# Graph attention layers 2 and 3: four heads projected ahead, the other pairs of heads projected inside the attention, and the order of its runs

## The chip, the cores and the metric

The kernel runs on one core of a Trainium2 chip. The metric is the device time in microseconds of one execution. The times shown are the median of three executions, and the profile is one further execution, recorded instruction by instruction. The engines of the core are TensorE (PE, matmuls and transposes, writing to PSUM), VectorE (DVE), ScalarE (ACT), GpSimd (POOL) and SyncE (SP, which only issues transfers). They run beside one another and wait for each other through semaphores; each takes its own instructions in order. Transfers are issued from the queues of SP, ACT and POOL.

## What is computed

Four graph layers over the same 2708 nodes with 512 features, each added to its input and layer-normalised. Layers 2 and 3 are graph attention (GAT) layers with eight heads of 64 features, and they are what the change touches:

```python
def _L2_gnn_ref(h, adj, W, a):                       # heads of layer 2; those of layer 3 are alike
    Wh = jnp.einsum('ni,hio->hno', h, W)             # [8 heads, 2708, 64]
    f1 = jnp.einsum('hno,ho->hn', Wh, a[:, :64])
    f2 = jnp.einsum('hno,ho->hn', Wh, a[:, 64:])
    e = jax.nn.leaky_relu(f1[:, :, None] + f2[:, None, :], 0.2)
    attention = jax.nn.softmax(jnp.where(adj[None] > 0, e, NEG_INF), axis=-1)
    h_prime = jnp.einsum('hnm,hmo->hno', attention, Wh)
    return jnp.transpose(h_prime, (1, 0, 2)).reshape(h.shape[0], 512)

x = _layernorm(x + layer2(x, adj))
# layer 3: elu(heads), then one attention with a single head of 512, elu, and an MLP 512 -> 1024 -> 512
x = _layernorm(x + layer3(x, adj))
```

All of it is float32. Layers 0 and 1 are aggregation layers without attention.

## The kernel before

The nodes are cut into 22 tiles of 128 rows (`NT`), the last with 20 rows. The program runs through stages: layers 0 and 1, then for each of layers 2 and 3 a projection (`project`) and the attention of its eight heads (`heads_attention`), then the projection, the attention and the MLP that end layer 3.

**The projection** (`project`, L588) goes tile by tile. It fetches 128 rows of x (`source`; for layer 3 that is `summed`, L950, which reads layer 2's heads from DRAM, scales them by the inverse divisors, adds the input, makes the layer norm and stores the result from POOL's queue, L961). PE turns them by four transposes (L131) and ACT copies the turned rows to SBUF (`xT`, L133; two buffers in the pool `ahead`). Then eight matmuls (L643), four slices of 128 features by two halves of the heads, accumulate into two PSUM tiles `pm` of 256 features and 8 more columns each: the halves' extra columns are the two attention scalars of each node. A float32 matmul is two instructions on PE, so a tile has 16 of them. From the scalars, DVE takes `dcol` and `b` (L648, L650), ACT makes the exponentials `ecol`, `ucol` (L664, L665) and `vcol` (L678), POOL makes `bcol` (L679), and PE turns `b` so that `v` can be stored as rows in DRAM (`keep_v`, L622 and L623). Two DVE instructions of 256 columns (L672) scale the features by `ecol` into `R2`, which stays in SBUF: [128 rows, 22 tiles, 512 features]. In the last six tiles, some of the first attention instructions are made ahead (`att.first`, L734: five in layer 2, four in layer 3).

**The attention** (`heads_attention`, L759) has eight runs. A run is a block of target nodes (11 tiles, 1408 columns, or the other 11, 1300 columns) by a pair of heads. The order before is block by block, and pair by pair within a block:

```python
runs = [(b, h0) for b in range(len(att.blocks)) for h0 in range(0, H, 2)]
```

At the start of a run SP loads `v` of each head, spread over the partitions (`v_bc`, L716, three buffers). The run has 22 steps, one for each tile j of neighbours. In a step DVE makes the masked weights e = max(v, u) * mask for each of the two heads (L722, five buffers, one instruction for each head, [128, 1408] or [128, 1300]); ACT makes from e the part above the leak's bend (`c`, L749, eleven buffers); and PE adds R2's features times e into `po` (L916), three PSUM tiles of up to 512 columns with the two heads on the two halves of the array's columns: 12 instructions a step. After every fourth step PE adds up the divisors from `c` (L818). In the first run of each block, the same sums are made once for the mask alone (`products`, L801, at steps 12, 16 and 20 of the run before it, or of the run itself for block 0). What is left of a run is spread over the first steps of the next (`finish`, the dictionary `todo`): the last divisors, folding them (L790), dividing (L840 to L845), and in layer 2 turning the heads to rows (L851) and storing them to DRAM in `o_dram` (L861 and after).[...]

PE's order is written out by hand: each instruction that goes through `pe()` is put behind the one before. The order on the other engines follows from a scheduler with the program's order as its priority, and from the pools: a tile's buffer is free when its last reader has ended. `summed` for the first two tiles and `elu_turned` (L966, the source of the projection after layer 3) for the first three can start while the attention still runs, since block 0 is complete after the fourth run; `elu_turned` is called from the last run's steps 9, 13 and 17.

## Time and profile before

| | us |
|---|---|
| median of three executions | 2957.79 (2957.10 to 2959.47) |
| span of the profiled execution | 2955.5 |
| layer 2: projection | 868 to 958 |
| layer 2: attention of the heads | 958 to 1504 |
| layer 3: projection | 1504 to 1608 |
| layer 3: attention of the heads | 1608 to 2155 |
| layer 3: the rest | 2155 to 2955 |

The stages' ends are read from the first and last instructions of their lines. The windows of these stages give the busy time of each engine:

```profile
core 0 of [0], span 2955.5 us
core 0: us, PE busy (x) PEld busy (x) DVE busy (x) ACT busy (x) POOL busy (x), PEclk, DMA share, GB/s
868.00:958.00 90.00, 89.73 (x453) 74.56 (x453) 37.48 (x122) 27.24 (x107) 9.20 (x31) 1.00 0.29 85
958.00:1504.00 546.00, 533.58 (x3782) 222.84 (x3781) 535.88 (x414) 508.44 (x412) 3.67 (x3) 1.00 0.12 40
1504.00:1608.00 104.00, 99.33 (x494) 79.05 (x493) 75.06 (x235) 45.42 (x135) 31.98 (x66) 0.97 0.55 178
1608.00:2155.00 547.00, 529.24 (x3723) 221.36 (x3721) 536.45 (x415) 509.60 (x399) 6.06 (x10) 1.00 0.12 41
```

After the stretch and its length, each pair is the busy time of an engine and (x) its number of instructions; PEld is PE's loading of weights, which goes on beside the matmuls. PEclk is the granted clock, DMA share the mean busy share of the 16 DMA engines. Two warnings for reading it. Matmuls are pipelined and their ends are modelled, so a busy PE need not be a PE at its limit; the time from one start to the next tells more. And the two attentions take 1093 of 2955 us; their runs, from one copy of the run's result (ACT, L926) to the next, last 75.7, 68.5, 69.8 and 73.0 us for block 0 of layer 2 and 63.9 to 65.5 us for block 1, and nearly the same in layer 3.

### The profile page before, as it was taken

The page shows a single profiled execution, that of the slowest core. Times are in us where ns is not written, and L with a number is a line of the kernel's source. Part 1 is how long each engine was busy: PE and PEld are TensorE (multiplying, and loading weights), DVE is VectorE, ACT ScalarE, POOL GpSimd, SP SyncE. Part 2 cuts the span into 40 slices and gives each one's busy share as a digit, 9 for nine tenths or more (in the row PEclk, how much of TensorE's full clock was granted, in tenths as well). Part 3 has the DMA queues.
Part 4 walks back from the last instruction along what each step waited for, and adds up shares of the span by engine and source line. Part 5 has one row for each costly group of instructions (what it writes and reads, how often), then busy time and mean ns, then how long its engine had stood idle before and what let it go on. Part 6 is the DMA issues. An engine that isn't in the chain of part 4 may idle for free. (4 is left out here: it accounts for less than half of the span.)

```text
span 2955.5 us, 36461 instructions
## 1 busy us (share of the span) xinstructions
PE 2874.1 (97%) x14398; PEld 1606.6 (54%) x14398; DVE 1998.5 (68%) x2408; ACT 1515.0 (51%) x1759; POOL 207.4 (7%) x344
## 2 busy tenths in 40 slices
PE   8999999999999999999999999999999999999998
PEld 4557766458888343444466433444475555555555
DVE  5866637543334999999977999999953434444342
ACT  3646532113223999999965999999951000000001
POOL 1101101101110000000022000000000010000001
PEclk9999999999999999999999999999999999999999
DMA  4633426322222111111143111121161000000000
GB/s 128 130 87 72 107 79 185 118 65 86 83 72 82 35 40 39 38 45 44 35 138 134 40 40 39 41 65 37 33 157 61 4 25 15 25 15 16 15 20 22
DMA packets 121152, 185.59 MB, mean 63 GB/s; under 512 B 41741, under 2 KB 66562, under 8 KB 120972
## 3 DMA queue, kind: packets, MB, share of 16 engines
q1 hardware_dynamic: 91808, 121.57, 13.8%
q0 software_dynamic: 18160, 57.39, 6.8%
q10 hardware_dynamic: 11004, 4.22, 0.6%
q8 instruction: 115, 1.88, 0.3%
q14 instruction: 65, 0.53, 0.1%
HBM read 153.10 MB, written 44.65 MB: 67 GB/s over the span
## 5 line engine op out<-in xcount | busy, mean ns | idle before, releaser
L722 DVE SCALAR_TENSOR_TENSOR e<-v_bc,ucol,maskT 128x1408 f32<-128x1408 f32 (+3 forms) x804 | 1135.9, 1469 | 327.6 <-PE pn L1097 314.4
L749 ACT ACTIVATE c<-e,bcol 128x1300 fp8e4<-128x1300 f32 (+1 forms) x688 | 965.8, 1423 | 65.4 <-DVE e L722 21.8
L916 PE MATMUL po<-e,R 128*64 128x512 f32 (+2 forms) x4224 | 907.8, 549 | 30.2 <-DVE e L722 27.3
L916 PEld LDWEIGHTS po<-e,R 128*64 128x64 f32 x4224 | 343.0, 137 | 561.9 <-issue 387.2
L1097 PE MATMUL pn<-e,R 128*128 128x512 f32 (+1 forms) x1056 | 413.4, 542 | 0.0
L1097 PEld LDWEIGHTS pn<-e,R 128*128 128x128 f32 x1056 | 191.0, 190 | 199.3 <-issue 196.1
L1048 ACT ACTIVATE w<-pl,b 128x256 f32<-128x256 f32 (+1 forms) x88 | 41.0, 466 | 372.8 <-PE pl L1046 364.7
L478 PE MATMUL acc<-yH,kT 128*128 128x512 f32 x484 | 197.4, 408 | 4.6 <-ACT kT L351 4.6
L478 PE MATMUL acc<-yL,kT 128*128 128x512 f32 x484 | 189.2, 391 | 0.0
L529 PE MATMUL acc<-yH,mf 128*128 128x512 f32 x484 | 188.4, 389 | 0.0
L529 PE MATMUL acc<-yL,mf 128*128 128x512 f32 x484 | 188.3, 389 | 0.0
L643 PE MATMUL pm<-w,xT 128*128 128x264 f32 (+1 forms) x704 | 167.5, 391 | 2.4 <-POOL ln_rs L120 0.8
L244 PE MATMUL pm<-weight,xT 128*128 128x512 f32 (+1 forms) x344 | 158.3, 603 | 7.6 <-DVE u L334 6.8
L1046 PE MATMUL pl<-lin 128*128 128x256 f32 (+1 forms) x704 | 153.4, 371 | 3.7 <-DVE lin L945 3.7
L120 POOL TENSOR_TENSOR ln_rs<-ln_rs,half 128x1 f32<-128x1 f32 (+1 forms) x88 | 55.1, 627 | 1447.1 <-DVE ln_rs L119 1378.6
L1071 PE MATMUL pl<-lin,w 128*128 128x512 f32 x336 | 150.8, 593 | 0.0
L1046 PEld LDWEIGHTS pl<-lin 128*128 128x128 f32 x704 | 129.1, 190 | 34.5 <-issue 15.8
L526 ACT CAST mf<-maskT 128x1024 fp32r<-128x1024 fp8e4 (+1 forms) x66 | 64.5, 977 | 156.5 <-PE acc L529 152.9
L643 PEld LDWEIGHTS pm<-w,xT 128*128 128x128 f32 (+1 forms) x704 | 129.2, 189 | 27.7 <-ACT xT L133 3.0
L244 PE MATMUL pm<-w,xT 128*128 128x512 f32 x296 | 135.3, 600 | 6.0 <-DVE yL L230 3.1
L351 ACT ACTIVATE kT<-maskT 128x512 fp32r<-128x512 fp8e4 (+1 forms) x132 | 77.5, 593 | 118.1 <-PE acc L478 118.1
L818 PE MATMUL pd<-c,parts_c 128*12 128x384 fp8e4 (+2 forms) x2752 | 128.3, 307 | 0.0
(239 smaller groups left out, 2635.4 us busy)
## 6 DMA issues: line engine op xcount, KB each, us to landing
rows<-x_dram SPq DMA_DIRECT2D x63, 256.0 KB
v_bc<-v_dram SPq DMA_DIRECT2D x16, 704.0 KB
rows<-in_x_dram SPq DMA_DIRECT2D x42, 256.0 KB
x_dram<-u POOLq DMA_DIRECT2D x42, 256.0 KB, 2.4
v_bc<-v_dram SPq DMA_DIRECT2D x16, 650.0 KB
m<-in_adj_dram POOLq DMA_DIRECT2D x13, 677.0 KB, 6.9
r_dram<-u POOLq DMA_DIRECT2D x21, 256.0 KB, 2.3
rows<-r_dram SPq DMA_DIRECT2D x21, 256.0 KB
```

The source lines that it names most:

```text
L244: order(nc.tensor.matmul(pm[:n], xT[:, k, :n], w[:, k, :], start=(k == 0), stop=(k == KD - 1)))
L351: made = nc.scalar.activation(kT[:, :w], maskT[:, j, b[0] * P:b[0] * P + w], AF.Relu, scale=-1.0)
L478: nc.tensor.matmul(pa[t], kT[:, (t - b[0]) * P:(t - b[0] + 1) * P], y[:, j, :], start=(j == 0 and y is yH), stop=(j == NT - 1 and y is yL))
L529: nc.tensor.matmul(pa, mf[:, j - g0, :], y[:, j, :], start=(j == 0 and y is yH), stop=(j == NT - 1 and y is yL))
L643: nc.tensor.matmul(pm[a][:m, :D // 2 + heads], xT[:, k, :m], w[:, k, a, :D // 2 + heads], start=(k == 0), stop=(k == KD - 1))
L722: self.made = nc.vector.scalar_tensor_tensor(e[:, :w], v[:, :w], ucol[:, j, h:h + 1], maskT[:, j, c0:c0 + w], op0=OP.max, op1=OP.mult)
L749: nc.scalar.activation(c[:, :w], e[:, :w], AF.Sigmoid, bias=bcol[:, j, h:h + 1], scale=STEP, saturate=False)
L818: pe(nc.tensor.matmul(p[32 * g:32 * g + 12, :c1 - c0], parts_c[:, j, h, :], c[:, c0:c1], start=(i == 0 and h == hs[0]), stop=(i == NT - 1 ...
L916: pe(nc.tensor.matmul(po[i][HO * k:HO * k + HO, :c1 - c0], R2[:, j, h * HO:(h + 1) * HO], e[:, c0:c1], start=(i_ == 0), stop=(i_ == NT - 1)))
L1046: nc.tensor.matmul(pl[:, :w], self.lin1[:, k, f * P:(f + 1) * P], h[:, k, :w], start=(k == 0), stop=(k == KD - 1))
L1071: nc.tensor.matmul(pl[:n], gT[:, f, (t - t0) * P:(t - t0) * P + n], self.lin2[:, f, :], start=(f == 0), stop=(f == KF - 1))
L1097: nc.tensor.matmul(pn[k][:, :w], R2[:, j, k * P:(k + 1) * P], e[:, :w], start=(j == 0), stop=(j == NT - 1))
```

## The change

For layers 2 and 3:

- `project` makes the features of heads 0 to 3 alone, with all sixteen attention scalars: one PSUM tile of 272 columns, four matmuls a tile (8 instructions), one scaling into `R2`. Half of the weights are loaded.
- Each tile's turned rows `xT` are stored to a new DRAM tensor `xT_dram`, from POOL's queue.
- The attention's runs go pair by pair: both blocks of heads 0 and 1, then both of heads 2 and 3, and so on. The sums of the masks are made in the first run for block 0 and in the second for block 1.
- The features of heads 4 and 5 are made during runs 1 to 3 and those of heads 6 and 7 during runs 4 to 6 (`projected`), in eight, eight and six tiles. For each tile SP loads its turned rows into a buffer (`rows`, three of them), PE makes four matmuls of 128 columns (8 instructions) at one of the steps 1, 3, 5, 7, 12, 14, 16, 18, and a DVE instruction scales four tiles at once from PSUM (512 columns) at step 11 and at the first step of the next run. The weights of the pair are loaded from SP at the first of the three runs.
- `ps_t` has one buffer instead of two; its bank goes to the features' PSUM tile `ps_p`.
- `elu_turned` for the first three tiles is called at steps 14, 17 and 20 of layer 3's last run.

Block 0 is now complete after the seventh run. In the order of instructions that follows, DVE's work of `summed` for the first two tiles lies at the start of layer 3's projection, where before it lay within layer 2's attention.

```diff
@@ -89,6 +89,11 @@
 
     o_dram = dram.tile([N, D], F32, name="o_dram")
     oT_dram, rc_dram = [], []
+    xT_dram = dram.tile([2, NT, P, KD * P], F32, name="xT_dram")
+
+    def turned_rows(layer, t, n):
+        return xT_dram[layer, t].rearrange("p (k n) -> p k n", k=KD)[:, :, :n]
+
 
 
 
@@ -592,12 +597,20 @@
 
         w = weight_tile()
         hh = max(heads // 2, 1)
-        for k in range(KD):
-            for a in range(2):
-                src = (w_src[4 * a:4 * a + 4, k * P:(k + 1) * P, :].rearrange("h p o -> p h o") if heads > 1 else
-                       w_src[k * P:(k + 1) * P, a * D // 2:(a + 1) * D // 2].rearrange("p (h o) -> p h o", h=1))
-                nc.scalar.dma_start(w[:, k, a, :D // 2].rearrange("p (h o) -> p h o", h=hh), src)
-        nc.gpsimd.tensor_copy(w[:, :, :, D // 2:D // 2 + heads], wa[:, layer, :, :, :heads])
+        half_d = D // 2
+        if heads > 1:
+            w = w.rearrange("p k a c -> p (k a c)")[:, :KD * (half_d + 2 * H)].rearrange("p (k c) -> p k c", k=KD)
+            for k in range(KD):
+                nc.scalar.dma_start(w[:, k, :half_d].rearrange("p (h o) -> p h o", h=hh),
+                                    w_src[:hh, k * P:(k + 1) * P, :].rearrange("h p o -> p h o"))
+            nc.gpsimd.tensor_copy(w[:, :, half_d:].rearrange("p k (i h) -> p k i h", i=2), wa[:, layer])
+            pieces = [w]
+        else:
+            for k in range(KD):
+                for a in range(2):
+                    nc.scalar.dma_start(w[:, k, a, :half_d], w_src[k * P:(k + 1) * P, a * half_d:(a + 1) * half_d])
+            nc.gpsimd.tensor_copy(w[:, :, :, half_d:half_d + heads], wa[:, layer, :, :, :heads])
+            pieces = [w[:, :, a, :half_d + heads] for a in range(2)]
         with ExitStack() as ph:
             sm = ph.enter_context(tc.tile_pool(name=f"{name}_s", bufs=2))
             ps_tr = ph.enter_context(tc.tile_pool(name=f"{name}_ptr", bufs=2, space=PSUM))
@@ -629,7 +642,9 @@
                 xT = xTs(t)
                 if t + 1 < NT:
                     xTs(t + 1)
-                pm = [ps_mm.tile([P, D // 2 + H], F32, name=f"pm{a}") for a in range(2)]
+                pm = [ps_mm.tile([P, half_d + 2 * H], F32, name=f"pm{a}") for a in range(len(pieces))]
+                s_ = pm[0][:, half_d:half_d + heads]
+                d_ = pm[0][:, half_d + H:] if heads > 1 else pm[1][:, half_d:half_d + heads]
 
                 twice = heads > 1 and t == LAST
                 if twice:
@@ -639,33 +654,33 @@
                     nc.gpsimd.memset(R2[TWIN:2 * TWIN, LAST, :], 0.0)
                 m = TWIN + n if twice else n
                 for k in range(KD):
-                    for a in range(2):
-                        nc.tensor.matmul(pm[a][:m, :D // 2 + heads], xT[:, k, :m], w[:, k, a, :D // 2 + heads],
+                    for a, piece in enumerate(pieces):
+                        nc.tensor.matmul(pm[a][:m, :piece.shape[2]], xT[:, k, :m], piece[:, k, :],
                                          start=(k == 0), stop=(k == KD - 1))
+                if heads > 1:
+                    nc.gpsimd.dma_start(turned_rows(layer, t, m), xT[:, :, :m])
                 if t:
                     keep_v(t - 1)
                 d = dcol[:n, t, :heads]
-                nc.vector.tensor_copy(d, pm[1][:n, D // 2:D // 2 + heads])
+                nc.vector.tensor_copy(d, d_[:n])
                 b = bs[t] = sm.tile([P, H], F32, name="b")
-                nc.vector.tensor_scalar(b[:n, :heads], pm[0][:n, D // 2:D // 2 + heads], -RANGE, RANGE,
-                                        op0=OP.max, op1=OP.min)
+                nc.vector.tensor_scalar(b[:n, :heads], s_[:n], -RANGE, RANGE, op0=OP.max, op1=OP.min)
...
                 else:
                     nc.scalar.activation(ecol[:n, t, :heads], d, AF.Exp, scale=ALPHA)
                     nc.scalar.activation(ucol[:n, t, :heads], d, AF.Exp, scale=1.0 - ALPHA)
                 with tc.issue_after(scaled[t - 1].ins) if first and t else nullcontext():
                     made = first(t) if first else None
-                for a in range(0 if twice else 2):
+                for a in range(0 if twice else len(pieces)):
...
@@ -756,7 +771,7 @@
         oT_dram.append(dram.tile([D, (z - a) * P], F32, name=f"oT_dram{i}"))
         rc_dram.append(dram.tile([H, 12 * P], F32, name=f"rc_dram{i}"))
 
-    def heads_attention(name, att, as_rows, exps, meanwhile={}):
+    def heads_attention(name, att, layer, exps, meanwhile={}):
 
 
 
@@ -764,14 +779,18 @@
         with ExitStack() as ph:
             ps_o = ph.enter_context(tc.tile_pool(name=f"{name}_po", bufs=4, space=PSUM))
             ps_d = ph.enter_context(tc.tile_pool(name=f"{name}_pd", bufs=1, space=PSUM))
-            ps_t = ph.enter_context(tc.tile_pool(name=f"{name}_pt", bufs=2, space=PSUM))
+            ps_t = ph.enter_context(tc.tile_pool(name=f"{name}_pt", bufs=1, space=PSUM))
+            ps_p = ph.enter_context(tc.tile_pool(name=f"{name}_pp", bufs=1, space=PSUM))
             sm = ph.enter_context(tc.tile_pool(name=f"{name}_sm", bufs=2))
+            as_rows, w_src = layer == 0, atts[layer][0]
             pd = [ps_d.tile([P, 512], F32, name=f"pd{i}") for i in range(2)]
             for p in pd:
                 nc.vector.memset(p, 0.0)
             Q = 3 * P
 
-            runs = [(b, h0) for b in range(len(att.blocks)) for h0 in range(0, H, 2)]
+            runs = [(b, h0) for h0 in range(0, H, 2) for b in range(len(att.blocks))]
+            later = list(range(H // 2, H, 2))
+            share = H // 2 * len(att.blocks) // 2 - 1
 
             def groups(b):
                 w = att.width(b)
@@ -885,6 +904,54 @@
                 return steps
 
 
+            def projected(i, r):
+
+                h0, step = later[i], r - i * share
+                got = {}
+                if step == 0:
+                    wp[i] = late.tile([P, D], F32, name="spare", bufs=2).rearrange("p (k c) -> p k c", k=KD)
+                    for k in range(KD):
+                        nc.sync.dma_start(wp[i][:, k, :].rearrange("p (h o) -> p h o", h=2),
+                                          w_src[h0:h0 + 2, k * P:(k + 1) * P, :].rearrange("h p o -> p h o"))
+                cols = slice(h0 * HO, (h0 + 2) * HO)
+                ts_ = range(8 * step, min(8 * step + 8, NT))
+                xs = early(1, len(ts_), lambda q: load(ts_[q]))
+
+                def load(t):
+                    m = TWIN + few if t == LAST else P
+                    xT = ahead.tile([P, D], F32, name="rows", bufs=3).rearrange("p (k n) -> p k n", k=KD)
+                    nc.sync.dma_start(xT[:, :, :m], turned_rows(layer, t, m))
+                    return xT[:, :, :m]
+
+                def make(q):
+                    if q % 4 == 0:
+                        got["ps"] = ps_p.tile([P, 4, P], F32, name="ps_p")
+                    xT = xs(q)
+                    m = xT.shape[2]
+                    for k in range(KD):
+                        pe(nc.tensor.matmul(got["ps"][:m, q % 4, :], xT[:, k, :], wp[i][:, k, :],
+                                            start=(k == 0), stop=(k == KD - 1)))
+
+                def scale(q0):
+                    a, z = ts_[q0], min(ts_[q0] + 4, NT)
+                    whole = min(z, LAST)
+                    ps = got["ps"].rearrange("p t (k o) -> p t k o", k=2)
+                    nc.vector.tensor_mul(R2[:, a:whole, cols].rearrange("p t (k o) -> p t k o", k=2), ps[:, :whole - a],
+                                         ecol[:, a:whole, h0:h0 + 2, None].to_broadcast([P, whole - a, 2, HO]))
...
+                steps = {}
+                for q in range(len(ts_)):
+                    steps[(1 if q < 4 else 12) + 2 * (q % 4)] = [lambda q=q: make(q)]
+                for q0 in range(0, len(ts_), 4):
+                    steps.setdefault(11 if q0 == 0 and len(ts_) > 4 else 22, []).append(lambda q0=q0: scale(q0))
+                return steps
+
+            wp = {}
             products, fold, keep = masks(0, pd[1])
             todo = {12: products[:1], 16: products[1:2], 20: products[2:], NT: [fold], NT + 2: [keep]}
             both = att.load_both(*runs[0])
@@ -896,6 +963,9 @@
                 vs = [att.load(b, h) for h in hs] if r else att.vs
                 po = [ps_o.tile([P, 512], F32, name="po", tag="po") for _ in parts]
                 pair = []
+                if r < len(later) * share:
+                    for j, steps in projected(r // share, r).items():
+                        todo[j] = todo.get(j, []) + steps
                 if r + 1 == len(runs):
                     for j, steps in meanwhile.items():
                         todo[j] = todo.get(j, []) + steps
@@ -928,8 +998,8 @@
                 todo = finish(b, h0, pd[r % 2], pair, oT, r + 1 == len(runs))
                 for j, steps in late_steps.items():
                     todo.setdefault(j - NT, []).extend(steps)
-                if h0 == H - 4 and b + 1 < len(att.blocks):
-                    products, fold, keep = masks(b + 1, pd[r % 2])
+                if r + 1 < len(att.blocks):
+                    products, fold, keep = masks(r + 1, pd[r % 2])
                     for j, steps in ((12, products[:1]), (16, products[1:2]), (20, products[2:]), (NT, [fold]), (NT + 2, [keep])):
                         todo[j] = steps + todo.get(j, [])
             for j in sorted(todo):
@@ -1132,8 +1202,8 @@
         with ExitStack() as ph:
             att = Weights(ph, f"a{2 + i}", blocks, vd[i], 5 - i)
             scaled = project(f"p{2 + i}", source, i, vd[i], blocks, first=att.first)
-            heads_attention(f"a{2 + i}", att, i == 0, scaled["v"], {
-                9 + 4 * t: [lambda t=t: ready.update({t: elu_turned(None, t, t + 1)})] for t in range(3)} if i else {})
+            heads_attention(f"a{2 + i}", att, i, scaled["v"], {
+                14 + 3 * t: [lambda t=t: ready.update({t: elu_turned(None, t, t + 1)})] for t in range(3)} if i else {})
     ph4 = fast.enter_context(ExitStack())
     att = Weights(ph4, "a4", quads, vd[2])
     lin = ph4.enter_context(tc.tile_pool(name="lin", bufs=1)).tile([P, KD * FF + KF * D + KD * 512], F32, name="lin")
```

## The prediction

> **What bounds the kernel now.** I read the page's slices first (which engine is full where), then windows inside the stages that the change touches, then the costliest groups of those windows with the waits beside them. The chain of waits names only the last 3 us of the program, so it carries nothing here.
>
> ```profile
> PE   8999999999999999999999999999999999999998
> DVE  5866637543334999999977999999953434444342
> ACT  3646532113223999999965999999951000000001
> DMA  4633426322222111111143111121161000000000
> ```
>
> ```profile
> core 0: us, PE busy (x) PEld busy (x) DVE busy (x) ACT busy (x) POOL busy (x), PEclk, DMA share, GB/s
> 885.00:945.00 60.00, 60.00 (x307) 50.92 (x306) 24.35 (x79) 18.21 (x71) 3.47 (x15) 1.00 0.32 95
> 1040.00:1100.00 60.00, 59.01 (x403) 24.46 (x401) 59.49 (x42) 55.27 (x41) 0.00 (x0) 1.00 0.13 41
> 1520.00:1590.00 70.00, 67.75 (x336) 54.71 (x335) 58.48 (x192) 32.66 (x95) 26.67 (x54) 1.00 0.68 222
> ```
>
> A slice is 74 us. PE shows a 9 everywhere, so the page alone doesn't tell what bounds what. DVE does: it is at 9 in two blocks (about 958 to 1504 and 1608 to 2155 us), which are the head attention of layers 2 and 3, and at 3 to 7 outside. The windows say the same closer up. In the projection of layer 2 (885 to 945) PE has no idle time while DVE, ACT and DMA are at 0.41, 0.30 and 0.32: PE bounds it. In attention (1040 to 1100) DVE is busy 59.49 of 60. In the projection of layer 3 (1520 to 1590) PE has 67.75 of 70, but DVE has 58.5 and DMA 0.68: two more bounds stand close behind.
>
> ```profile
> L643 PE MATMUL pm<-w,xT 128*128 128x264 f32 x237 | 55.2, 386 | 0.0
> ...
> L131 PE MATMUL ps_tr<-ident,rows 128*128 128x128 f32 x56 | 8.4, 273 | 0.0
> L672 DVE TENSOR_TENSOR R<-pm,ecol 128x256 f32<-128x256 f32 x30 | 11.3, 420 | 4.7 <-ACT ecol L664 4.7
> ...
> ...
> DVE b L650 <- PE pm L643: 27.0, 13, 2.4
> ```
>
> ```profile
> L722 DVE SCALAR_TENSOR_TENSOR e<-v_bc,ucol,maskT 128x1408 f32<-128x1408 f32 x39 | 62.8, 1678 | 0.0
> L916 PE MATMUL po<-e,R 128*64 128x512 f32 (+1 forms) x246 | 54.1, 563 | 1.0 <-DVE e L722 1.0
> ...
> PEld po L916 <- DVE e L722: 6.1, 11, 1.3
> ```
>
> The first of these fences is of 885 to 945, its last line from the waits: PE idles 0.0 us ahead of its matmuls, while DVE waits 27 us for them. The second is of 1035 to 1100: 39 of the e instructions fill 62.8 of 65 us (1.61 each, start to start 1.595) with no idle before them, while PE waits for e (6.1 us on its weight loads).
>
> **What the Trainium skill says.** "Trainium Kernel Development and Optimization" (Performance Expectations) calls matmul busy time a bad metric, because matmuls are pipelined. The trace agrees: L916 lasts 563 ns in the row, yet the 12 of one step (a neighbour tile, two heads) take 2.36 us, 0.197 each, when PE is late and has all its inputs. So I count PE in start-to-start times. "TensorE: Matmul & The Clock Gate" (Back-to-back issue gap) says that the spacing in a stream of loads and matmuls is set by both; its section on LDWEIGHTS gives P/1.2 ns, 107 for 128 columns. In the trace, a 128x128 float32 load with 128 columns (L131) goes at 0.109 us, with 16 columns (L790) at 0.111, and with 264 columns (L643) at 0.2225. "Trainium Kernel Development and Optimization" (Key Constraints) says that transfers of all queues run on the same 16 DMA engines; so the new stores go into one account with the loads of layer 3's projection.
>
> **Layer 2's projection.** A tile now: 16 x 0.2225 = 3.56, four transposes 0.44, one 8-column turn 0.11, sum 4.11 us, which is the measured period (880.01 to 884.12). After: four matmuls of 272 columns in one bank, 8 instructions; 0.2225 x 272/264 = 0.229, so 8 x 0.229 + 0.55 = 2.38. Saving 1.73 x 22 = 38 us if PE goes on bounding. DVE falls to some 1.25 us a tile (24.35/60 x 4.11 less one R2 scale of 0.42), ACT stays at 1.25, so nothing else is over 2.38. New is the store of turned rows: xT has two buffers, and the copy of tile t+2 waits until tile t has left. By the order of instructions on POOL, the store of tile t+1 stands behind tile t-1's bcol, so it is issued some 1.3 us into tile t; POOL's 256 KB stores landed 2.4 us (x_dram<-u) and 3.5 us (x3's rows) after issue, so it has left 3.7 to 4.8 us into tile t. Tile t+3 comes 3 x 2.38 = 7.1 us into it and its copy takes 0.58: the store fits by 1.7 to 2.8 us. At the start and end, where the pipeline fills, nothing is saved. I take -34 (-22 if the stores wait 0.5 us a tile, -38 at most).
>
> **Layer 3's projection.** From 1508 to 1608 now: 100 us. After: PE 22 x 2.38 = 52. DVE 70.7 (1510 to 1600) less 22 x 0.42, plus 4.8 for the first two tiles' residual and layer norm (for each three 512-wide instructions of 0.68 to 0.69 and three small ones), which before ran inside the attention of layer 2 (its runs 4 to 6) and now, since block 0 is done only after the seventh run, come at the projection's head: 66. DMA: 17.6 MB (1510 to 1600) plus 22 x 0.25 MB = 23.1; 222 GB/s at a share of 0.68 makes 326 GB/s when full: 71 us. So something near 71 bounds, plus 5 us of latency until the first tile is turned, plus 5 of friction between three resources that are all over 0.6: 81. That is -19 (-32 with the bound itself and no latency, -5 if the chain rows, store, pow on POOL's one queue sets the pace).
>
> **Attention, what is added.** Six of eight runs get 8, 8 or 6 tiles of features each. A tile is 8 instructions of 128 columns, at 0.109 to 0.111, plus some 0.2 for switching between half and full columns of the array: 1.1 us; 8.8 us a run. PE's own work in a run, counted start to start, is 55.6 to 64.9 of 63.9 to 75.7 us. So the runs that get it come to: first run 62.9 + 8.8 = 72 of 75.7; second 60 + 8.8 and, since both blocks' masks (1.3 to 1.5 us a group) now lie in the first two runs, 65 + 8.8 = 74; the others 64 to 69 of 64 to 70. PE is then at 94 to 100%. DVE gets two scales a run (512-wide from PSUM; 0.69 from other 512-wide rows; 0.42 for half the width speaks for 0.68): 12 x 0.68 = 8.2 a layer, all of it on the bound; a gain is excluded, since e instructions run without a gap. The transfers (5.5 MB a layer out, 5.5 x 2 back, three buffers, a share of 0.13 now) are covered, since SP issues the loads a run ahead.
>
> What can't be read is the stall from clumping. The makes lie at steps 1, 3, 5, 7 and 12, 14, 16, 18, in one stretch with the turns of the run before. PE's slack is 0.46 us a step (3.19 less 2.36 and shares of the divisors); steps 0 to 8 give 4 us of slack and ask 4.4 plus 2 of turns. PE falls 2 to 3 us behind; e has 5 buffers, 2.5 steps, so DVE is stopped only when PE is more than about 3 us late. Least: none (less than nothing isn't possible, nothing is taken from DVE here but the layer norms counted above). Most: 2.5 us at both clumps of each run, 5 us a run. I take 1.5 a run on the mean, 11 us in layer 2 (with its turns to rows) and 7 in layer 3 (without them). So layer 2: +8.2 + 11 - 4.8 (the layer norms moved out) = +14; layer 3: +8.2 + 7 = +15. That the runs go pair by pair costs the loads of v nothing by count: 16 of each width as before. The ELU work at the end of layer 3 is the same work; before, part of it stood in three earlier runs, on DVE in either case.
>
> **Sum.** -34 - 19 + 14 + 15 = -24 us of the profiled execution's 2955.5, 2931.5; the median of the runs shown is 2.3 us above it: 2934.
>
> **Rivals.**
> A, no stall: PE's slack takes it all, the rings smooth the clumps. For it: L916 at 12 in 2.36 against 3.19. Then -34 - 19 + 3.4 + 8.2 = -41: 2916.
> B, PE becomes attention's bound: each of the 12 loaded runs loses 5 us where I took 1.5, because PE at 94 to 100% with makes in clumps is late whenever e's ring is full, and DVE's later work is never made up. One number decides: the savings (53) less scales (16.4) plus 4.8 leave 41 us, so 3.5 us a run is the break-even. At 5 us: -41 + 60 = +19, 2977. It would also come about from a make of 1.5 us in place of 1.1. Against it: 128-column matmuls went at 0.11, not at 0.2.
> C, the projections keep their times: the two-deep xT ring with a store on it, and DMA in layer 3, take back half. -20 - 8 + 29 = +1 at worst; I put it at -25 - 8 + 29 = -4: 2954.
>
> **Chances.** Forecast 0.50, A 0.17, B 0.20, C 0.13. What a measurement can tell from no change is about 0.2%, 6 us. Faster: 0.50 + 0.17 + 0.05 of C = 0.72; the rest of C is no change, 0.08; B is slower, 0.20. The likeliest case alone spans 2918 to 2950 (stalls from 8 to 30, projections by the bounds above). The range takes in A and most of C and the nearer part of B: 2906 to 2968.
>
> **What will show it.** Layer 2's projection in some 56 us at a tile period of 2.4, PE still without gaps; if DVE's b waits for something other than the matmuls, or the copy of xT waits for DMA, C is right. Layer 3's in about 80, DMA share near 0.9. In attention: the new matmul's group at 0.11 start to start; waits of e for PE's attention matmuls (po), hardly any before, give the stall directly: under 0.3 us a run is A, over 3.5 is B. Runs 7 and 8 of each layer have no makes and should keep 65 us. Wrong would be: a first run over 80 us, or a stall at the runs' starts where v's load now stands behind the loads of turned rows on SP.

## The result, and the profile after

The changed kernel took 2966.98 us (median of five executions, 2965.38 to 2971.48) against 2957.67 for the kernel before (five executions): a ratio of 1.0034, with a 95% interval of 1.0022 to 1.0047. It is slower, by some 9 us. 2934 had been forecast, and a range of 2906 to 2968.

The windows of the four stages in the profile after, to set beside those of before (after the stretch and its length, busy time and number of instructions of each engine; then PE's granted clock, the DMA engines' share and GB/s):

```profile
core 0 of [0], span 2963.6 us
...
867.00:924.00 57.00, 52.26 (x277) 41.38 (x275) 26.92 (x99) 24.93 (x105) 25.97 (x52) 1.00 0.74 232
924.00:1494.00 570.00, 562.53 (x4138) 252.86 (x4141) 544.44 (x427) 506.16 (x413) 1.74 (x2) 1.00 0.19 58
1494.00:1596.00 102.00, 72.81 (x319) 48.71 (x311) 68.30 (x220) 45.10 (x138) 52.25 (x89) 0.88 0.74 242
1596.00:2164.00 568.00, 555.38 (x4073) 246.96 (x4073) 545.12 (x427) 508.29 (x399) 6.02 (x10) 1.00 0.19 58
```

Layer 2's projection has lost a third of its time. Both attentions have grown, and their DVE, which was busy 536 of 546 us, now is idle for 26 of 570. Layer 3's projection is as long as before, though PE is busy in it for 73 us and no longer for 99. Its lost PE time has become idle time.

The stages, in us, each from the end of the one before: the first projection from its first matmul, a projection to its last matmul, an attention to its last copy of a run's result. The first column holds what the sum of the prediction had for the change; the last three are runs described below:

| stage | predicted | before | after | order alone | no scales | half makes |
|---|---|---|---|---|---|---|
| layer 2: projection | -34 | 89.8 | 57.3 | 89.8 | 65.5 | 59.0 |
| layer 2: attention | +14 | 546.5 | 570.5 | 547.2 | 569.7 | 555.7 |
| layer 3: projection | -19 | 103.9 | 101.2 | 103.8 | 105.1 | 101.2 |
| layer 3: attention | +15 | 546.5 | 568.2 | 552.5 | 569.0 | 560.3 |
| layer 3: projection behind it | 0 | 81.9 | 85.7 | 87.7 | 86.5 | 86.3 |

(The run without scales clears half of R2 on POOL at the head of both projections, 4.8 us each, and these two stages are longer in it.)

The five stages together: 14.3 us longer. What lies around them isn't touched by the change: layers 0 and 1 end 1.7 us earlier and the last attention with the MLP is 4.5 us shorter, which leaves the span 8.1 us longer. Over all runs below these two vary by themselves (864.5 to 869.5 us, and 713.4 to 722.5 us), and the second varies with PE's granted clock in it: 713.4 to 713.5 us in the four runs that had 0.997 there, 722.5 in the one that had 0.986. So the runs are compared by their stages; where a whole time matters, several executions were taken.

The waits of DVE in layer 2's attention, of before and then of after (what waited, for what: us in total, times, longest):

```profile
DVE e L722 <- ACT c L749: 2.8, 1, 2.8
DVE e L722 <- DMA v_bc<-v_dram: 2.1, 3, 0.9
DVE e L722 <- PE po L916: 1.1, 2, 0.7
```

```profile
DVE e L737 <- PE po L986: 16.4, 19, 2.4
DVE e L737 <- DMA v_bc<-v_dram: 5.1, 6, 1.3
DVE e L737 <- ACT c L764: 2.7, 1, 2.7
```

The first line of the second is the new wait: e has no free buffer because PE hasn't yet multiplied with it (`po`), 16.4 us where it was 1.1. In layer 3's attention the same wait is 12.4 us:

```profile
DVE e L737 <- PE po L986: 12.4, 17, 2.0
```

### The profile page after: what moved, and what is told of

It is laid out like the page before. It is cut to its first block, busy times and chain, and to the rows that moved or that the text cites. A ratio compares the mean times of both kernels' runs of the same rounds, so it can differ in the third digit from the quotient of the medians.

```text
span 2963.6 us, 37418 instructions
## 1 busy us (share of the span) xinstructions
PE 2867.9 (97%) x14750; PEld 1601.5 (54%) x14750; DVE 1999.3 (67%) x2394; ACT 1508.3 (51%) x1759; POOL 242.5 (8%) x388
## 5 line engine op out<-in xcount | busy, mean ns | idle before, releaser
L986 PE MATMUL po<-e,R 128*64 128x512 f32 (+2 forms) x4224 | 875.5, 547 | 17.4 <-DVE e L737 13.2
L986 PEld LDWEIGHTS po<-e,R 128*64 128x64 f32 x4224 | 314.3, 136 | 511.0 <-issue 398.8
L1188 ACT COPY lin<-pn 128x512 f32<-128x512 f32 (+1 forms) x12 | 6.4, 535 | 209.3 <-PE pn L1167 209.3
L234 ACT CAST yH<-pm 128x512 fp32r<-128x512 f32 x33 | 19.3, 585 | 182.0 <-PE pm L249 182.0
```

Source lines behind the costliest of these rows:

```text
L986: pe(nc.tensor.matmul(po[i][HO * k:HO * k + HO, :c1 - c0], R2[:, j, h * HO:(h + 1) * HO], e[:, c0:c1], start=(i_ == 0), stop=(i_ == NT - 1)))
```

## The experiments

The line numbers in the fences are those of each run's own program.

### The order alone, and the scales alone

The kernel before with the order of runs changed and nothing else of the change:

```diff
-            runs = [(b, h0) for b in range(len(att.blocks)) for h0 in range(0, H, 2)]
+            runs = [(b, h0) for h0 in range(0, H, 2) for b in range(len(att.blocks))]
-                if h0 == H - 4 and b + 1 < len(att.blocks):
-                    products, fold, keep = masks(b + 1, pd[r % 2])
+                if r + 1 < len(att.blocks):
+                    products, fold, keep = masks(r + 1, pd[r % 2])
-                9 + 4 * t: [lambda t=t: ready.update({t: elu_turned(None, t, t + 1)})] for t in range(3)} if i else {})
+                14 + 3 * t: [lambda t=t: ready.update({t: elu_turned(None, t, t + 1)})] for t in range(3)} if i else {})
```

> The kernel before with the new order of runs alone (pair by pair, both masks in the first two runs, the turned rows of the last stage from step 14 on); all eight heads projected ahead as before. Theory M (the features made on PE cost the attention its time): each layer's attention within 4 us of the 546.5 of before, the end of layer 3's projection about 4 us later than before for the layer norms that move into it. Rival O (the order itself costs, by the loads of v and by the masks): attention longer by 10 us or more in each layer, of the 24 and 22 that the change added.

Measured: attention of layer 2 at 547.2 (+0.7), of layer 3 at 552.5 (+6.0), the projection behind it at 87.7 (+5.8). One execution took 2968.87 us, and one of the kernel before beside it 2956.89. Theory M holds for layer 2's attention, and both theories missed layer 3's. The 4 us that theory M expected in layer 3's projection for the layer norms that move there didn't come (103.8 against 103.9). The order costs 12 us at layer 3's end, and the timeline of DVE there shows why (start, length, line, what is made):

```profile
2145.03 0.43 DVE L992 TENSOR_SCALAR xT<-xT 128x512 f32<-128x512 f32 x1
...
2146.85 0.69 DVE L993 SCALAR_TENSOR_TENSOR rows<-rows,xT 128x512 f32<-128x512 f32 x1
...
2150.42 0.69 DVE L990 TENSOR_TENSOR rows<-rows,spare 128x512 f32<-128x512 f32 x1
...
2155.04 0.43 DVE L992 TENSOR_SCALAR spare<-spare 128x512 f32<-128x512 f32 x1 [0.96 <-ACT spare L991]
```

These are `elu_turned`'s instructions for the first tiles of the last stage. Here its work begins on DVE at 2129.5 us, near the end of the last run; before, two of the three tiles were begun at 1955, three runs earlier, since block 0 was complete. With the order alone DVE waits 0.9 to 1.5 us for v, or for ACT's copy of the run before, at the start of each of layer 3's runs; before, the starts of the last three runs show no such wait, and the early work stands there (1955, 2021 and 2086 us). Pair by pair, block 0 is complete only when one run is left.

The same shows in layer 2. The prediction had subtracted 4.8 us for the layer norms of two tiles that leave the attention. They left it, and the attention grew by 0.7: DVE's waits for v went from 2.1 to 5.3 us in their place:

```profile
DVE e L722 <- DMA v_bc<-v_dram: 5.3, 6, 1.1
...
DVE e L722 <- PE po L916: 2.8, 3, 1.2
```

The second run is the changed kernel without the DVE scaling of the features made inside (the features of heads 4 to 7 stay zero):

```diff
+            nc.gpsimd.memset(R2[:, :, half_d:], 0.0)
...
-                for q0 in range(0, len(ts_), 4):
-                    steps.setdefault(11 if q0 == 0 and len(ts_) > 4 else 22, []).append(lambda q0=q0: scale(q0))
```

> The changed kernel without the DVE instructions that scale the features made inside the attention (the features of heads 4 to 7 stay zero); PE makes them as in the change. Theory M: DVE's 12 scales a layer are worth their own 8 us, and the rest of the added 24 and 22 us stays: attention about 16 and 14 us over before. Rival S (the scales sit in DVE's queue waiting for PE, and this is what stops e): attention within 6 us of before, and the waits of e for PE gone.

Measured: 569.7 and 569.0 us, within 0.8 of the changed kernel. Both theories missed. Taking 8 us of work from DVE gave nothing back, and the wait for PE grew by about 3 us:

```profile
DVE e L738 <- PE po L985: 19.3, 21, 2.4
DVE e L738 <- DMA v_bc<-v_dram: 9.0, 7, 2.1
```

So DVE isn't the bound of these runs any more. The makes alone, without any scale, account for the whole 22.5 us over the order.

### Half of each make

If PE is full, half of the makes' time should bring DVE back to being the bound, and then the scales should show.

```diff
-                    for k in range(KD):
+                    for k in range(KD // 2):
                         pe(nc.tensor.matmul(got["ps"][:m, q % 4, :], xT[:, k, :], wp[i][:, k, :],
-                                            start=(k == 0), stop=(k == KD - 1)))
+                                            start=(k == 0), stop=(k == KD // 2 - 1)))
```

> The changed kernel, but each tile's features made inside the attention take only the first two of their four matmuls (half of the sum over the inputs is left out); loads, scales, places and order are the change's. Theory P (PE full; it had some 4.4 us free in a run, the makes take 8.5, so that only the rest is paid): with 4.3 us in place of 8.5 the stall nearly goes, attention of layer 2 at 553 to 557 (547.2 with the order alone, 8 of scales on DVE now uncovered), the waits of e for PE small. Rival M (each make costs its own half of a microsecond wherever it stands): 559, half way.

Measured: layer 2's attention 555.7, inside theory P's range; layer 3's 560.3, half way between 552.5 and 568.2, which alone would fit theory M as well. The runs that have makes and no masks, the third to the sixth, keep the masks and the stages' ends out of it. Their sum in layer 2 is 269.3 us with the order alone, 282.0 with the change, 281.5 without its scales, and 273.4 with half makes and all scales. Whole makes cost 12.2 us without the scales and the scales another 0.5, which can't be told from nothing (seven runs with the change's attention had 280.9 to 282.5). Half makes and scales cost 4.1 together, 2.3 of it one wait for ACT's copy, where the four runs' eight scales of 0.7 us are 5.5 of DVE work. In layer 3 the same four runs take 269.9 with the order alone, 275.8 with the change and 271.6 with half makes, less than half way too; what brought its attention to half way is in the first two runs. What waits for PE in the half run:

```profile
DVE e L737 <- PE po L986: 4.8, 5, 1.7
```

All five of these waits lie in the first two runs, where the masks are. Outside them PE has just enough time for half of the makes, and not for all.

### How full PE is

The windows of the fourth run (block 1, no masks), of the order alone and then of the change:

```profile
1170.00:1234.00 64.00, 62.61 (x447) 26.66 (x447) 62.83 (x48) 59.91 (x50) 0.00 (x0) 1.00 0.14 45
```

```profile
1149.00:1219.00 70.00, 70.00 (x523) 33.00 (x521) 67.12 (x51) 61.82 (x50) 0.00 (x0) 1.00 0.23 72
```

The first number pair after the length is PE, the third DVE. PE is at 70.00 of 70 and DVE has lost 3 us. As a busy PE proves little, here are the groups of PE in the changed kernel's window 1150 to 1219 (last column: idle time before the group):

```profile
L986 PE MATMUL po<-e,R 128*64 128x512 f32 (+2 forms) x266 | 52.2, 532 | 0.0
L932 PE MATMUL ps_p<-spare,rows 128*128 128x128 f32 x64 | 9.1, 285 | 0.0
L837 PE MATMUL pd<-c,parts_c 128*12 128x384 fp8e4 (+2 forms) x172 | 8.0, 303 | 0.0
L870 PE MATMUL ps_t<-ident,oT 128*128 128x128 f32 x11 | 1.9, 288 | 0.0
```

No group waits for anything. Counted from start to start over this run: 52.1 us of attention (270 matmuls at 0.193), 8.5 of makes (64 at 0.133), 7.6 of divisors (172 at 0.044), 1.5 of turns and 0.8 of folding, 70.4 in all, and the run lasts 70.6. A run has 264 of the attention's matmuls (PE was late, so six of the run before fall into this one), 50.9 us. A part of these 50.9 is due to the makes too. One attention step between other groups takes 2.33 us in this run, two in a row take 4.51 (once 4.73) and four 8.88: that is 2.18 a step and 0.15 for each stretch. The run has 13 stretches of attention where the order alone has 7, so the makes add some 0.9 us to the 8.5 of their own. PE's work without them is then some 60 us, in a run that lasts 65.2 with the order alone: PE had some 5 us to spare and was asked for 9.4. Half makes take 4.9 us in this run and just fit, as the section before shows.

### Fewer makes

Six heads ahead and one pair inside, in at most five tiles a run:

```diff
         half_d = D // 2
         if heads > 1:
+            half_d, hh = 3 * D // 4, 3 * heads // 4
...
-            later = list(range(H // 2, H, 2))
-            share = H // 2 * len(att.blocks) // 2 - 1
+            later = [H - 2]
+            counts = (2, 2, 4, 5, 5, 4)
+            share = len(counts)
...
-                    steps[(1 if q < 4 else 12) + 2 * (q % 4)] = [lambda q=q: make(q)]
+                    steps[3 + 4 * q] = [lambda q=q: make(q)]
```

> Six heads are projected ahead and one pair is made inside the attention, in 2, 2, 4, 5, 5 and 4 tiles of runs 1 to 6, one every fourth step; order of runs as in the change. Layer 2's projection is then 22 x (8 x 0.337 + 0.55) = 71 us. Theory P (PE is full in the loaded runs; its free time before was some 4.4 us a run, four tiles' worth, and only what goes beyond is paid): attention of layer 2 at 549 to 553, that is at most 6 us over the run with the order alone (547.2), by its scales. Rival M (every tile made there costs its half microsecond, as 23 us for 44 tiles did): 558 or more.

Measured: projection 72.1, as worked out. Attention 559.0, above both: but 4.9 us of it are two waits at the starts of the fifth and sixth runs (2.6 and 2.3 us, both put down to ACT's copy of the run before), which the order alone hasn't. Layer 3's attention has 556.0, 3.5 over the order alone, 2.7 of it one wait for v: there theory P fits, and half of the 15.7 that 44 makes cost, 7.9, is not reached. In layer 2 the size of the make's own cost isn't settled by this run.

The next has another order, in which block 0 is complete after the sixth run:

```diff
-            runs = [(b, h0) for h0 in range(0, H, 2) for b in range(len(att.blocks))]
+            runs = [(b, h0) for i in range(0, H, 4) for b in range(len(att.blocks)) for h0 in (i, i + 2)]
-            counts = (2, 2, 4, 5, 5, 4)
+            counts = (5, 5, 3, 5, 4)
...
```

> As the run with six heads, with another order: block 0 and then block 1 of the first two pairs, then block 0 and then block 1 of the last two, so that block 0 is complete after the sixth run; 5, 5, 3, 5 and 4 tiles in the first five runs; the turned rows of the last stage at steps 9, 13 and 17 as before. Theory P, with block 0's early end giving back what the order alone cost (6.0 in layer 3's attention, 5.8 in the projection behind it): attention of layer 3 at 548 to 553, the projection behind it at 82; the whole about 2950. Rival (the order's cost isn't block 0's late end): these two stay at 552 or more and 86 to 88, the whole at 2960 or more.

Measured: the projection behind layer 3's attention back at 83.3 (82 expected), layer 3's attention at 557.7 (548 to 553 expected), its last run at 68.0 in place of 70.8. So block 0's late end was most of the order's cost in the projection behind; what it cost layer 3's attention isn't told apart from the makes here. The whole took 2956.36 us in one execution. Attention of layer 2 was 560.9, with waits of 2.3 and 2.1 us for v at the starts of two runs.

### Layer 3's projection

Seven runs look for what holds this stage at 101 us. In the first the store of layer 3's turned rows is cut to 4 of 512 columns, its place in POOL's queue kept (layer 3's attention loads layer 2's turned rows instead; this second edit isn't shown). In the second the store goes to another queue, in the third the store of x3:

```diff
-                    nc.gpsimd.dma_start(turned_rows(layer, t, m), xT[:, :, :m])
+                    if layer:
+                        nc.gpsimd.dma_start(xT_dram[1, t, :, :4], xT[:, 0, :4])
+                    else:
+                        nc.gpsimd.dma_start(turned_rows(layer, t, m), xT[:, :, :m])
...
-                    nc.gpsimd.dma_start(turned_rows(layer, t, m), xT[:, :, :m])
+                    nc.scalar.dma_start(turned_rows(layer, t, m), xT[:, :, :m])
...
-        nc.gpsimd.dma_start(x3_dram[t * P:t * P + n, :], x3)
+        nc.scalar.dma_start(x3_dram[t * P:t * P + n, :], x3)
```

> In layer 3's projection the store of the turned rows is cut to 4 of 512 columns, and layer 3's attention loads layer 2's turned rows instead (other data of the same size). The instruction stays in its place in POOL's queue. Theory D (the bytes: 23 MB in layer 3's projection at some 300 GB/s): that stage falls from 101 us, counted from the last copy of layer 2's attention, to about 85. Rival Q (POOL's one queue: the store waits there for ACT's copy of xT, and the power for the next layer norm stands behind it): 97 or more, hardly changed.

> The store of turned rows is issued from ACT's queue instead of POOL's, in both layers; the same bytes. Rival Q: layer 3's projection falls from 101 to about 85 us. Theory D: 97 or more. Layer 2's projection stays near 57 us in both, unless ACT's queue is stopped by the issue of the stores.

> The changed kernel with one line changed: layer 3's projection stores the layer norm's rows (x3) from ACT's queue instead of POOL's; the turned rows still go from POOL's. Theory K (POOL's queue makes a ring: the power of a tile's layer norm, DVE, ACT's rows, the store of x3 that waits for them, and only then the power of the next tile): the stage falls from 101 us, counted from the last copy of layer 2's attention, to 85 to 90. Rival L (latency and order of DVE's queue, or DMA, bound it): 97 or more.

Measured: 97.8, 102.6 and 99.3 us. The bytes are worth 3.4; taking a store from POOL's queue gave -1.4 (the turned rows) and 1.9 (x3). Theories D, Q and K all fall as the main cause. x3 on ACT's queue was tried with the mixed order too:

> The run before it with x3 stored from ACT's queue too. With theory K: layer 3's projection 10 us or more shorter than in that run, so about 2940, 17 us below the kernel before. With rival L: the same time as that run.

It had this stage at 98.0, 4.5 below the mixed order's 102.5 and not 10, and the whole at 2961.42 us (12 executions; ratio to before 1.001, 1.0001 to 1.0019), 21 above what theory K expected.

SP issues the loads of this stage when a buffer comes free, so the depth was tried next:

```diff
-        o = fetched(o_dram, t, n) if t < 2 else fetched(o_dram, t, n, sm, "o", 3)
-        x2 = fetched(x2_dram, t, n, late, "spare", 2)
+        if 2 <= t < NT - 6:
+            ring = att.pool.tile([P, att.W], F32, name="e", bufs=5)
+            o, x2 = ring[:n, :D], ring[:n, D:2 * D]
+            nc.sync.dma_start(o, o_dram[t * P:t * P + n, :])
+            nc.sync.dma_start(x2, x2_dram[t * P:t * P + n, :])
+        else:
+            o = fetched(o_dram, t, n) if t < 2 else fetched(o_dram, t, n, sm, "o", 3)
+            x2 = fetched(x2_dram, t, n, late, "spare", 2)
```

> The changed kernel; in layer 3's projection the rows of layer 2's heads and of its input for tiles 2 to 15 are loaded into the five buffers of e, which are idle there, where they had three and two. Theory R (SP issues each load when a buffer comes free, the load takes 4 to 6 us, and this ring sets the pace): the stage falls from 101 us to 90 or less, DVE's waits for these loads go. Rival L (the layer norm's chain through DVE, POOL, ACT and PE in a fixed order sets it): 98 or more.

> The changed kernel with both: the five buffers for layer 3's loads, and x3 stored from ACT's queue. Theory N (several bounds close behind one another, loads, POOL's queue, bytes: taking away one uncovers the next): the stage falls below 92, more than the 6.5 and 1.9 us of the two alone would add up to (92.8). Rival L (the tile's chain through DVE, ACT and PE in a fixed order is the bound): 93 or more.

> As the run before it, and the store of the turned rows in layer 3's projection cut to 4 of 512 columns (layer 3's attention loads layer 2's turned rows instead). Theory N: near 80, since DVE's 66 us and PE's 52 us are the next bounds. Rival L: 90 or more.

Measured: 94.7, 96.3 and 93.4 us. The first lies between its two theories; in the other two the stage doesn't come below 93, as rival L said. But these times add up two parts that moved against each other. Here are PE's first matmuls of the stage in the changed kernel, which begins at 1494.4 us:

```profile
1500.30 3.90 PE L658 MATMUL pm<-w,xT 128*128 128x272 f32 x16
...
1511.61 3.09 PE L658 MATMUL pm<-w,xT 128*128 128x272 f32 x6 [0.67 <-ACT xT L138]
```

The first line is the first two tiles, which were ready; the third tile begins at 1511.6. So in us from the stage's start, and for the 20 tiles from the third on:

| | third tile begins | the other 20 tiles | one of them |
|---|---|---|---|
| before | 17.7 | 86.1 | 4.3 |
| changed | 17.2 | 84.0 | 4.2 |
| store cut | 17.2 | 80.6 | 4.0 |
| turned rows stored from ACT's queue | 16.8 | 85.8 | 4.3 |
| x3 on ACT's queue | 17.3 | 82.0 | 4.1 |
| five buffers for the loads | 21.7 | 72.9 | 3.6 |
| five buffers, x3 on ACT's queue | 22.0 | 74.3 | 3.7 |
| five buffers, x3 on ACT's queue, store cut | 21.0 | 72.4 | 3.6 |

Before, PE's own 4.11 us was close to a tile's time. With that gone, the depth of the loads held the tiles at 4.2: five buffers take 11 us off the 20, and theory R holds for this part. It isn't only work done earlier, in a longer head: the last 14 tiles alone fall from 59.5 to 51.1. 4.5 of the 11 are lost at the head, where the loads now come ten at a time and the DMA engines are at a share of 0.99 (1505 to 1525 in the first of the three runs); that this delays the third tile is likely, but wasn't tried apart. The depth of the loads is thus the largest cause that these runs show. Once the loads are deep, neither the bytes nor POOL's queue is worth anything more (74.3 and 72.4 against 72.9).

What holds the tiles at 3.6 then is less clear. In the last run no engine is full (window 1510 to 1585; PE, PEld, DVE, ACT, POOL):

```profile
1510.00:1585.00 75.00, 54.61 (x252) 38.77 (x253) 61.95 (x197) 38.38 (x116) 31.82 (x61) 0.92 0.67 207
```

and every engine waits for another one (same stage, 1510 to 1585):

```profile
POOL ln_rs L125 <- DVE ln_rs L124: 24.2, 13, 4.1
ACT rows L130 <- DVE ln_mv L129: 19.1, 16, 5.0
PEld ps_tr L136 <- ACT rows L130: 13.7, 11, 6.3
...
ACT xT L138 <- PE ps_tr L136: 7.0, 8, 1.9
...
DVE ln_mv L129 <- POOL ln_rs L125: 4.0, 10, 0.9
...
DVE dcol L668 <- PE pm L658: 3.2, 6, 1.3
```

The lines make a circle: DVE to POOL (the power), POOL to DVE, DVE to ACT (the rows), ACT to PE (the turns), PE to ACT (xT), PE to DVE (dcol). DVE carries three of these hops for several tiles in one fixed order. PE's share of it hardly matters with the loads as shallow as before: with eight, six and four heads projected here the stage took 103.9, 102.5 to 105.2, and 101.2 us, while PE's own work fell from 22 x 4.11 = 90 over 22 x 3.25 = 71 to 22 x 2.38 = 52. Which hop would have to go wasn't tried, so that the circle holds the tiles at 3.6 is argued from these waits, not shown by a run.

### A version that is faster than both

With six heads, mixed order, five buffers and the turned rows loaded from POOL's queue (idle in the attention), in 4, 5, 4, 5 and 4 tiles:

```diff
-                    nc.sync.dma_start(xT[:, :, :m], turned_rows(layer, t, m))
+                    nc.gpsimd.dma_start(xT[:, :, :m], turned_rows(layer, t, m))
```

> The mixed order with six heads ahead, with the five buffers of e for layer 3's projection, the turned rows loaded from POOL's queue in place of SP's, and 4, 5, 4, 5 and 4 tiles in the first five runs. If SP's one queue held up the loads of v behind those of turned rows (2 us at the starts of four runs of the mixed order): attention of both layers 4 us or more shorter than in the mixed order's run (560.9 and 557.7). With theory R: layer 3's projection at 90. Then about 2938; with neither about 2956.

Measured: attentions of 558.4 and 555.2, 2.5 each below the mixed order, not 4; layer 3's projection 99.8, where theory R had 90 (its 20 tiles take 78.0 in place of the mixed order's 86.1, but the third begins at 21.7 in place of 16.4); the whole 2954.04 us against 2957.32 (ratio 0.9992, 0.9983 to 1.0001), not told from the kernel before. Then the same in layer 2 alone, layer 3 being left as it was (and its loads as shallow):

```diff
+        inside = heads > 1 and layer == 0
-        if heads > 1:
+        if inside:
...
+            wide = 4 if layer == 0 else H
-            runs = [(b, h0) for i in range(0, H, 4) for b in range(len(att.blocks)) for h0 in (i, i + 2)]
+            runs = [(b, h0) for i in range(0, H, wide) for b in range(len(att.blocks)) for h0 in range(i, i + wide, 2)]
-            later = [H - 2]
+            later = [H - 2] if layer == 0 else []
```

> The inside features in layer 2 alone: six heads ahead, one pair made in the first five runs (4, 5, 4, 5, 4 tiles), mixed order, turned rows loaded from POOL's queue; layer 3 is projected and attended to as in the kernel before. If layer 3's projection isn't bound by PE, taking work from PE there gains nothing and its attention pays: so layer 3 keeps its 732 us of before (projection, attention, projection behind it; 738 in the run with both layers changed) and layer 2 gains 18 in its projection and pays 12 in its attention: 2951, 6 us below before. If layer 3's change had paid for itself: 2954 or more.

Measured: 2945.69 us (five executions, 2941.51 to 2949.86) against 2956.50: a ratio of 0.9964, 0.9950 to 0.9977. Layer 2's projection takes 71.9 and its attention 557.3 (18 gained, 11 paid), layer 3's three stages 105.0, 546.6 and 83.9, as before within 3.2 us together. So the five stages account for 3.9 of the 11.7 us by which its profiled execution is shorter. The other 7.8 lie in the stages around them, which no edit touches. A part of this goes with the granted clock, 0.997 in the mean of its five executions and 0.995 in those before; over 40 executions of the kernel before, 0.001 more clock went with 1.6 us less, which makes some 3 us as an estimate. The rest stays open, so some 4 us is what the profile shows of the version's own gain. The windows of the first two:

```profile
865.00:936.00 71.00, 69.98 (x276) 41.27 (x274) 30.19 (x98) 24.69 (x104) 24.09 (x55) 1.00 0.62 197
936.00:1494.00 558.00, 548.81 (x3975) 237.33 (x3973) 540.25 (x422) 509.10 (x413) 12.82 (x22) 1.00 0.16 48
```

PE is still full in the projection, and DVE is at 540 of 558 in the attention, half way between the 536 of 546 of before and the 544 of 570 of the change.

## Why the prediction was wrong

**Layer 2's projection: right.** -34 was taken, -32.5 came. PE bounded it still: 16 of the 21 steps from tile to tile took 2.38 or 2.39 us, as the sum had it. The stores weren't quite free, though the sum had let them fit: seven of ACT's copies waited for one to land, and one of these waits reached PE, for 2.7 us.

```profile
ACT xT L138 <- DMA xT_dram<-xT: 9.0, 7, 4.0
```

**Layer 3's projection: the step "something near 71 bounds, plus latency and friction: 81" failed.** The stage came to 101. The sum took the largest of the engines' loads as the bound, and left some 5 us each for latency and friction, or up to 14 more for the chain through POOL's queue. Counted as in the table, its third tile would have begun at some 15 us (3.5 to 1508, 5 of latency, two tiles' share of 71), which was 17.2; and the other 20 tiles would have taken 69.5 (their share of 71, and 5 of friction), which was 84.0. The friction is the term that was mis-sized, by 14.5 us. What it left out is the time that a load takes and how few can be on their way: with five buffers these tiles took 72.9. The prediction had the bounds "close behind" PE from busy shares alone; by its own prices PE needed 22 x 4.11 = 90 of the 104 us before, and the shallow loads held the tiles at 4.2 us right behind that. Why 3.6 us a tile are left with deep loads stays open. (The range's end of -32 doesn't come out of its own figures: 100 less 71 is 29.) The remark of the Trainium skill that the prediction itself quoted ("Trainium Kernel Development and Optimization", Performance Expectations: matmul busy time is a bad metric) held for this stage too, and it had been applied to the attention alone.

**PE in the attention: the mechanism was rival B's, and the term that failed is "PE's own work in a run".** The make's price was right: 1.1 us forecast, 1.09 measured (8.5 to 8.7 a run). PE's work without makes was put at 55.6 us and up, the low end for runs of block 1; the account above gives some 60 for such a run. Some 50 of it are the attention's matmuls, where the prediction's 2.36 us a step, scaled from 1408 to 1300 columns, makes 47.9. That was a step in the middle of a stretch of equal instructions. The make's price held 0.2 for the change between half and full columns of the array; not priced was what each such change costs on the attention's side, 0.15 us a stretch. The Trainium skill ("TensorEngine Tiling (Array Packing)", Key Properties) says that a change of tiling mode drains the engine; the trace agrees: eight matmuls of a make take 1.089 us between attention matmuls where 8 x 0.111 is 0.89, and a step that stands alone between other groups takes 2.33 us, one of two in a row 2.26. With some 5 us of spare time where 55.6 had left 8 or more, the makes cost 23.3 us in layer 2 and 15.7 in layer 3 over the order, scales included; 19 and 15 had been set for stalls and scales. In layer 2 that is short by 4. In layer 3 it is right to a microsecond, but by luck: it had 8 us of scales that didn't show, and 7 of stall where the waits for PE came to 12.4.

**The scales: priced at 8.2 us a layer on the bound, and worth nothing there.** Without them layer 2's attention is 0.8 us shorter and layer 3's 0.8 longer: PE is the bound in the loaded runs, and they are hidden behind it.

**The order: "the same work" was the error.** The layer norms and ELUs that run early were priced by their DVE time wherever they stand. Before, part of them stood where DVE otherwise waits for v. Moved, the 4.8 us that the attention of layer 2 was to gain didn't come, and layer 3's end paid 6.0 in the attention and 5.8 behind it with the order alone (of the second, 3.8 in the changed kernel). That makes 15 us that the sum didn't have.

**The rivals.** A, no stall, is refuted by the 16.4 and 12.4 us of waits for PE. C named the right stage and the wrong cause in layer 3: neither the ring of two xT buffers (1.4 us of waits, 1510 to 1590) nor the bytes (3.4) took the gain. B had the mechanism and the sign of the whole, but not the size: it put 5 us on each loaded run beside 16 of scales, 76 in all, where 39 came, and the waits for PE were 2.7 and 2.1 us a run, under its own mark of 3.5. The sum turned because B's 41 us of margin weren't there: 16 of them were lost in layer 3's projection and 15 in the order.

**The signs it named.** A first run of over 80 us was to mean wrong, and it took 80.6 in layer 2 (79.1 in layer 3). The waits for v at the runs' starts grew from 2.1 to 5.1 us in layer 2, but the order alone has 5.3. The runs without makes didn't both keep 65 us: the seventh is now one of block 0, and took 70.5 (70.3 with the order alone), the eighth 64.0.

## What to carry to other kernels

Before giving an engine more work, add up what it does from start to start over a whole stage, with the changes between kinds of work in it, and compare that with the stage's length; a busy share of 95% and a price from the middle of a stretch both hide how little is left. Before taking work from an engine, look for what comes next behind it, and count the buffers of the loads among the candidates: here layer 2's projection gave the time back, and layer 3's didn't, because shallow loads stood right behind PE. Read a stage's head apart from its steady part, or a gain in one hides behind a loss in the other. And when a reordering ends a block later, look for what was filling the gaps behind its early end.

## What was not expected of the hardware

The DMA engines' share alone didn't tell how long a transfer takes. The turned rows, 256 KB from POOL's queue, landed 2.7 us after issue in layer 2's projection and 4.0 in layer 3's (medians), at shares of 0.74 (867 to 924) and 0.78 (1500 to 1590). The rows of layer 2's heads on which DVE waited came 2.7 to 4.7 us after their issue before, and 3.5 to 8.6 after. Why wasn't tried.

PE's granted clock was 0.88 in layer 3's projection, where PE was busy for 73 of 102 us (before: 0.97, with 99 of 104 busy). A matmul of 272 columns there has a mean of 444 ns, against 396 for one of 264 before.
